# Seven weight blocks of a 1024x1024 layer pair at seven places modulo 512 bytes

## The chip, the core and the metric

The kernel runs on one core of a Trainium2 chip. The metric is device time in microseconds (us) of one execution; three runs of the kernel before gave 335.15, 336.11 and 336.05 us, so the median is 336.05. The profile is one further execution under the hardware profiler.

TensorE (PE in the profile) multiplies. Each of its matmuls has a stationary operand, which a separate LDWEIGHTS instruction reads from SBUF (engine PEld in the profile), and a moving operand, which streams out of SBUF while the matmul runs. VectorE is DVE, ScalarE is ACT, GpSimd is POOL; SP issues most of the small transfers and POOL those of the weights.

## What is computed

The input x is 8 batches of 256 rows of 256 values, with a context of 120 rows per batch.

```python
x = x + xattn(layernorm(x), ctx, ctx, ctx)      # gelu(x c^T) * (x c^T) @ c
n = layernorm(x)
h = silu(n @ w1.T * s1) * (n @ w2.T * s2)       # 256 -> 1024, twice
h = gelu(h @ h1.T * s_h1)                       # 1024 -> 1024
h = gelu(h @ h2.T * s_h2)                       # 1024 -> 1024
x = x + h @ w3.T * s3                           # 1024 -> 256
```

All five weight matrices are ternary (-1, 0, 1), with one scale for each output column. The 2048 rows are worked on as NT = 4 tiles of N = 512 rows, rows in the free dimension.

## The kernel before

**Stages.** Batch by batch, attention and the second layernorm give xT (lines 275 to 285 are its matmuls). `gated` (L438) multiplies xT by the stationary block `w12`. Then come four calls of `hidden` (L514), two for each 1024x1024 layer, each for two tiles of 512 rows; last `output` (L560) multiplies by `w3`, and finish_rows (L308, L309) scales and adds the residual.

**Exact activations.** An activation block is split in two fp32r parts, hi (rounded by ACT, L483) and lo = q - hi (DVE, L487), and each product is done twice, once with each part. In `operand` the two parts stand in a ring of RING = 3 slots: hi0, lo0, hi1, lo1 in the pool "middle", hi2, lo2 in the pool "later".

**Seven products instead of eight.** `hidden` is a 2x2 block scheme of the Strassen-Winograd kind. A layer's weight is four 512x512 blocks "11", "12", "21", "22" and three sums of them, s1, s2, s4, which DVE makes in place (`sum_weights`, L359). Each of these seven stationary blocks belongs to one of the seven products of ORDER, and lies in one of seven SBUF tiles `wt[0]` to `wt[6]`, named w0 to w6; HOME says which, for each layer. A tile is 128 partitions of 4x4x128 fp32 values, that is 8192 bytes on each partition. A product is 4 output groups `m` of 8 matmuls, 4 with hi and 4 with lo, each with a stationary slice of 128x128 and a moving slice of 128x512:

```python
def product(p, slot, m, bank):
    w = weight(layer, WEIGHT[p])
    for kind, part in enumerate(slot_views(slot)):
        for k in range(4):
            nc.tensor.matmul(
                mm[bank], lhsT=w[:, m, k, :], rhs=part[:, k, :],
                start=(p in OPENS and kind == 0 and k == 0),
                stop=(p in CLOSES and kind == 1 and k == 3), skip_group_check=True)
```

So a call has 7 x 4 x 8 = 224 matmuls, the four calls 896, and every weight tile is the stationary operand of 128 of them. In `output` the roles turn: slices of hi and lo are stationary, `w3` moves, 256 columns at a time.

**Order of the work.** Every operation goes into a `Plan` with an engine, a cost and its reads and writes; a list scheduler with fixed seeds (PICKS) sets the order on each engine before the program is built. It knows costs and dependences, not addresses. The loads of the second layer's blocks (L351, on POOL) wait until the products that read the tile before are done.

**Where the tiles lie.** The pool "keep" is filled in the order of its lines: q0 to q7 (8192 bytes each), w0 to w6, d0 to d3, w32; the pools of attention, and later "middle", begin behind it. "early" (w12, xT) and "later" (hi2, lo2, w3, o, x1) lie at the right end. Three constants pad: ALIGN = 16 fp32 values ahead of "keep", ALIGN_W3 = 8 ahead of w3, ALIGN_RIGHT = 112 at the end of "later". In the built program q0 starts at byte 8192 of a partition and w0 at 73728. Modulo 512 bytes, which this text calls the *place* of a tile (a stationary slice of 128 fp32 values is 512 bytes, a moving slice of 512 is 2048, so all slices of a tile share its place):

| tiles | place before |
|---|---|
| w0 to w6 | 0 for all seven |
| hi0, hi1, hi2, lo0, lo1, lo2 | 0 |
| w12 and xT | 480 |
| w3 | 32 |
| d0 to d3 | 0; `bad`, with which DVE combines them (L379), 384 |

Of the kernel before, what the change touches and what calls it, by code (L numbers as in the profile page):

```python
# [10 lines left out]
F32 = mybir.dt.float32  # L11
F32R = mybir.dt.float32r
# [8 lines left out]
P = 128  # L21
# [21 lines left out]
)  # L43
ALIGN, ALIGN_W3, ALIGN_RIGHT = 16, 8, 112
ATT, LOADS = 4, 6
FORCE_GENERAL = False

FIRST = (range(2), range(2, 4))
# [125 lines left out]
def xattn_ffn_kernel(ctx: ExitStack, tc: tile.TileContext, x, ctx_b, wall, scal, s3, out):  # L174
# [137 lines left out]
    with ExitStack() as es, ExitStack() as wide:  # L312
        open_pool = lambda stack, name, **kw: stack.enter_context(
            tc.tile_pool(name=name, bufs=1, **kw))
        keep = open_pool(es, "keep")
# [3 lines left out]

        mm = [psum.tile([P, N], F32, name=f"mm{i}") for i in range(8)]  # L320
        q = [keep.tile([P, 4, N], F32, name=f"q{i}") for i in range(8)]
        wt = [keep.tile([P, 4, 4, P], F32R, name=f"w{i}") for i in range(7)]
        d = [keep.tile([P, 1024], BF16, name=f"d{i}") for i in range(4)]
        w32 = keep.tile([P, 1024], F32, name="w32")
        x1s = dram.tile([NB * S, D], F32, name="x1s")
# [274 lines left out]
        for c in (0, 2):  # L600
            plan.dma("POOL", 0.8, lambda c=c: load_w12(c), 1.05, r=[("first", 0, 0)],
                     w=[("w12", c), ("w12", c + 1)], chain="weights")
# [80 lines left out]

    with tc.If(inexact == 0 if FORCE_GENERAL else inexact != 0):
        with ExitStack() as es:
# [8 lines left out]
            for c in range(NCH):  # L694
                w = wpool.tile([P, 1024], F32, tag=f"g{c}", name=f"g{c}")
# [90 lines left out]
```

## Time and profile before

| | before |
|---|---|
| median of 3 runs | 336.05 us |
| the profiled execution's own time | 334.57 us |
| its span, first to last instruction | 332.7 us |
| mean granted TensorE clock | 0.990 |
| PE busy | 318.5 us, 96% |
| PEld busy | 274.0 us, 82% |
| DVE busy | 257.5 us, 77% |
| ACT busy | 214.8 us, 65% |
| POOL busy | 52.8 us, 16% |

Busy time of PE is the union of pipelined matmuls: a matmul with 512 moving columns is shown as 389 ns long, though the next one starts well before its end. What a matmul costs in a dense stretch is the distance from start to start, and this text calls it the *pitch*. It is had by dividing a stretch's length by the number of matmuls in it. The chain of work that ended last gives such stretches with their counts.

### The profile page before, as it was taken

The page shows a single profiled execution, that of the slowest core. Times are in us where ns is not written, and L with a number is a line of the kernel's source. Part 1 is how long each engine was busy: PE and PEld are TensorE (multiplying, and loading weights), DVE is VectorE, ACT ScalarE, POOL GpSimd, SP SyncE. Part 2 cuts the span into 40 slices and gives each one's busy share as a digit, 9 for nine tenths or more (in the row PEclk, how much of TensorE's full clock was granted, in tenths as well). Part 3 has the DMA queues.
Part 4 walks back from the last instruction along what each step waited for, and adds up shares of the span by engine and source line. Part 5 has one row for each costly group of instructions (what it writes and reads, how often), then busy time and mean ns, then how long its engine had stood idle before and what let it go on. Part 6 is the DMA issues. An engine that isn't in the chain of part 4 may idle for free.

```text
span 332.7 us, 4563 instructions
## 1 busy us (share of the span) xinstructions
PE 318.5 (96%) x1670; PEld 274.0 (82%) x1670; DVE 257.5 (77%) x410; ACT 214.8 (65%) x316; POOL 52.8 (16%) x93
## 2 busy tenths in 40 slices
PE   3599999999999999999999999999999999999993
PEld 2399999988888888888888888888888888889993
DVE  5777778788998758997577998966997855747984
ACT  2457777558389777676777875688668656664510
POOL 4273141020015031111012210022003000000000
PEclk9989999999999999999999999999999999999997
DMA  7969700020059519509848860019006200002542
GB/s 220 384 204 340 254 33 33 32 95 3 0 176 115 58 10 149 97 14 223 204 97 221 122 155 9 0 12 109 8 0 69 27 0 2 0 0 66 146 126 87
DMA packets 22382, 32.44 MB, mean 97 GB/s; under 512 B 1744, under 2 KB 15184, under 8 KB 22352
## 3 DMA queue, kind: packets, MB, share of 16 engines
q0 software_dynamic: 10256, 17.30, 27.9%
q1 hardware_dynamic: 12096, 14.77, 14.3%
q8 instruction: 15, 0.25, 0.3%
q14 instruction: 15, 0.12, 0.1%
HBM read 33.64 MB, written 4.19 MB: 114 GB/s over the span
## 4 chain that ended last, share of the span: by engine, by line
PE 95%; DVE 1%; POOL 1%; DMA 1%; issue 0%; SPq 0%; ACT 0%; POOLq 0%
PE mm L514 61%; PE mm L438 18%; PE mm L560 9%; PE mm L275 2%; PE mm L285 2%; PE mm L280 2%; POOL ln_rs L252 1%; DMA xb<-x_d 1%; DVE ln_st L241 0%; DVE xn L263 0%; DVE o L308 0%; DVE xb L301 0%; DVE o L309 0%; DVE ge L298 0%; SPq L207 0%
## 5 line engine op out<-in xcount | busy, mean ns | idle before, releaser
L514 PE MATMUL mm<-hi,w 128*128 128x512 f32 x448 | 119.7, 389 | 0.0
L514 PE MATMUL mm<-lo,w 128*128 128x512 f32 x448 | 119.7, 389 | 0.0
L487 DVE TENSOR_TENSOR lo<-q,hi 128x1024 fp32r<-128x1024 f32 x72 | 86.3, 1220 | 17.1 <-ACT hi L483 17.0
L514 PEld LDWEIGHTS mm<-lo,w 128*128 128x128 f32 x448 | 84.1, 188 | 17.5
L514 PEld LDWEIGHTS mm<-hi,w 128*128 128x128 f32 x448 | 84.1, 188 | 17.4
L483 ACT CAST hi<-q 128x1024 fp32r<-128x1024 f32 x72 | 72.7, 1046 | 11.1 <-PE mm L560 8.2
L438 PE MATMUL mm<-xT,w 128*128 128x256 f32 (+1 forms) x384 | 65.8, 326 | 0.0
L438 PEld LDWEIGHTS mm<-xT,w 128*128 128x128 f32 x384 | 56.5, 191 | 5.4
L529 DVE TENSOR_TENSOR q<-q,mm 128x512 f32<-128x512 f32 x48 | 32.9, 687 | 28.7 <-PE mm L514 27.7
L533 ACT ACTIVATE q<-q,sc 128x512 f32<-128x512 f32 x48 | 34.2, 722 | 23.2 <-DVE q L529 22.8
L377 POOL DMA_DIRECT2D d<-wall_d x22 | 24.6, 1141 | 118.8 <-ACT d L375 118.8
L523 ACT COPY q<-mm 128x512 f32<-128x512 f32 x48 | 28.1, 587 | 22.8 <-PE mm L514 21.9
L459 ACT ACTIVATE q<-mm,sc 128x256 f32<-128x256 f32 (+1 forms) x48 | 25.9, 546 | 19.3 <-PE mm L438 19.0
L506 DVE TENSOR_TENSOR q<-q,q 128x1024 f32<-128x1024 f32 x32 | 38.2, 1218 | 0.0
L461 DVE SCALAR_TENSOR_TENSOR q<-q,sc,mm 128x256 f32<-128x256 f32 (+1 forms) x48 | 26.3, 560 | 3.6 <-ACT q L459 2.1
L375 ACT ACTIVATE d<-w 128x1024 bf16<-128x1024 f32 x22 | 23.0, 1057 | 0.0
L359 DVE TENSOR_TENSOR w<-w,w 128x512 fp32r<-128x512 f32 x32 | 20.8, 683 | 0.0
L560 PE MATMUL mm<-w,hi 128*128 128x256 f32 x128 | 20.2, 280 | 0.0
L560 PE MATMUL mm<-w,lo 128*128 128x256 f32 x128 | 20.1, 279 | 0.0
L275 PE MATMUL mm<-ident,xn 128*128 128x128 f32 x64 | 11.2, 298 | 7.7 <-DVE xn L263 7.7
L560 PEld LDWEIGHTS mm<-w,hi 128*128 128x128 f32 x128 | 17.2, 188 | 0.1
L560 PEld LDWEIGHTS mm<-w,lo 128*128 128x128 f32 x128 | 17.2, 188 | 0.0
(47 smaller groups left out, 181.0 us busy)
## 6 DMA issues: line engine op xcount, KB each, us to landing
w<-wall_d POOLq DMA_DIRECT2D x11, 1024.0 KB, 8.8
d<-wall_d POOLq DMA_DIRECT2D x22, 256.0 KB, 6.3
w<-wall_d SPq DMA_DIRECT2D x8, 512.0 KB, 4.0
x<-x1s SPq DMA_DIRECT2D x16, 128.0 KB, 2.8
out_d<-o SPq DMA_DIRECT2D x16, 128.0 KB, 1.9
cb<-ctx_d SPq DMA_DIRECT2D x8, 248.0 KB, 5.7
xb<-x_d SPq DMA_DIRECT2D x7, 256.0 KB, 7.2
x1s<-xb SPq DMA_DIRECT2D x7, 256.0 KB, 2.9
```

Of the source, the lines that this page charges most:

```text
L377: plan.dma("POOL", 0.8, lambda: nc.gpsimd.dma_start(d4, src, accum_op=ALU.add), 1.04, w=[("d", i)], lag=8.0)
L438: nc.tensor.matmul(sides[side], lhsT=w12[:, m // 2, (((m % 2) * 2 + side) * 2 + k) * P :][:, :P], rhs=xT[t % 2][i][:, k, cols], start=firs ...
L459: add("ACT", act(n, 1), lambda o=o, b0=b0, m=m: nc.scalar.activation(o, b0, AF.Silu, scale=sc[:, m : m + 1]), r=[("mm", banks[0]), "sc", " ...
L461: add("DVE", dve(n) + 0.05, lambda o=o, b1=b1, m=m: nc.vector.scalar_tensor_tensor(o, o, sc[:, 8 + m : 9 + m], b1, op0=ALU.mult, op1=ALU.m ...
L483: nc.scalar.copy(slot_views(i)[0][:, ms], q[src][:, ms])
L487: nc.vector.tensor_sub(l[:, ms], q[src][:, ms], h[:, ms].bitcast(F32))
L506: add("DVE", dve(1024), lambda ms=ms: nc.vector.tensor_tensor(q[into][:, ms], q[x][:, ms], q[y][:, ms], op=ALU.subtract), r=q_keys(x, ms) ...
L514: nc.tensor.matmul(mm[bank], lhsT=w[:, m, k, :], rhs=part[:, k, :], start=(p in OPENS and kind == 0 and k == 0), stop=(p in CLOSES and kin ...
L523: add("ACT", act(512), lambda: nc.scalar.copy(q[i][:, m], mm[bank]), r=[key], w=[("q", i, m)])
L529: add("DVE", dve(512), lambda: nc.vector.tensor_tensor(o(), o(), mm[bank], op=ALU.add), r=[key], w=[("q", i, m)])
L533: add("ACT", act(512, 1), lambda: nc.scalar.activation(o(), src(), AF.Gelu, scale=sc[:, col : col + 1]), r=["sc", "table"] + ([] if p in a ...
L560: nc.tensor.matmul(mm[banks[j]][:, :D], lhsT=part[:, k, j * P : (j + 1) * P], rhs=later["w3"][:, r, k * D : (k + 1) * D], start=(r == 0 an ...
```

## The change

The tiles w0 to w6 get small pads ahead of them, so that their places modulo 512 bytes become 0, 64, 128, 192, 256, 320 and 448. A last pad of 64 bytes fills up to 512, so that every tile behind them moves by exactly 512 bytes and keeps its place.

```diff
 ATT, LOADS = 4, 6
+OFF = (0, 64, 128, 192, 256, 320, 448)
 ...
         q = [keep.tile([P, 4, N], F32, name=f"q{i}") for i in range(8)]
-        wt = [keep.tile([P, 4, 4, P], F32R, name=f"w{i}") for i in range(7)]
+        wt = []
+        for i, off in enumerate(OFF):
+            if off:
+                keep.tile([P, (off - OFF[i - 1]) // 4], F32, name=f"off{i}")
+            wt.append(keep.tile([P, 4, 4, P], F32R, name=f"w{i}"))
+        keep.tile([P, (512 - OFF[-1]) // 4], F32, name="off7")
         d = [keep.tile([P, 1024], BF16, name=f"d{i}") for i in range(4)]
```

The order of the instructions on all five engines, and what they wait for, is the same in both programs; only addresses differ. The pads are never written or read.

## The prediction

> **What bounds the kernel now.** I read the chain of work that ended last first, since PE is busy 96% of the span and the question is what a matmul costs. From 63 us it reads:
>
> ```profile
> 63.15 3.64 PE mm L438 x16
> 66.79 0.86 PE mm L285 x4
> 67.66 5.47 PE mm L438 x24
> 73.13 0.44 PE mm L275 x4
> 73.57 1.86 PE mm L438 x8
> 75.43 0.44 PE mm L275 x4
> 75.86 18.18 PE mm L438 x80
> 94.04 203.12 PE mm L514 x896
> 297.16 22.40 PE mm L560 x192
> ```
>
> Columns: start, length in us, engine and line, number of instructions. The 896 matmuls that read the moved blocks are one unbroken piece of 203.12 us, 61% of the span: PE waits for nothing in it, and a matmul costs its pitch, 203.12 / 896 = 226.7 ns. The 80 matmuls of the same shape in L438 take 227.2 each, the eight ahead of them 1.86 / 8 = 232.5. L560, with half as many columns, takes 22.40 / 192 = 116.7 ns; L438 with 256 columns, from an earlier piece of the same chain, 4.79 / 40 = 119.8:
>
> ```profile
> 42.64 4.79 PE mm L438 x40
> ```
>
> The timeline of PE at the seam of L438 and L514 (start, length, then form and count):
>
> ```profile
> 93.64 0.40 PE L438 MATMUL mm<-xT,w 128*128 128x512 f32 x1
> 93.88 1.08 PE L514 MATMUL mm<-hi,w 128*128 128x512 f32 x4
> 94.80 1.08 PE L514 MATMUL mm<-lo,w 128*128 128x512 f32 x4
> 95.72 1.07 PE L514 MATMUL mm<-hi,w 128*128 128x512 f32 x4
> 96.62 1.07 PE L514 MATMUL mm<-lo,w 128*128 128x512 f32 x4
> ```
>
> Starts 0.92, 0.92, then 0.90 us apart for four: the first eight cost (95.72 - 93.88) / 8 = 230 ns, the later ones 226. Nothing is waited for here. What differs is one passage: while the last L438 matmul streams from place 480, the first slice of w0, at place 0, is being loaded. The next eight have hi0, lo0 and w0 all at 0 and still need a while to find the steady pitch. The last view is the group of that line:
>
> ```profile
> L514 PEld LDWEIGHTS mm<-hi,w x448: 187/188/188, 93.6 to 295.6; 128*128 128x128 f32 x150
> L514 PE MATMUL mm<-hi,w x448: 387/389/398, 93.9 to 295.9; 128*128 128x512 f32 x150
> ```
>
> Minimum, median, maximum in ns. A long one shows a long pitch: the 398 belongs to those first eight. So the trace holds unsettled matmuls from 2 ns under to 9 ns over the steady ones.
>
> **The change part by part.** No instruction, wait, queue entry or DMA is added, removed or reordered; only addresses change. So the sum has one main term: matmuls of L514 times the change of their pitch. w0 keeps place 0; six tiles move, each stationary in 4 calls x 4 groups x 8 = 128 matmuls, 768 in all. While such a matmul streams hi or lo from place 0, the next slice of the same tile is loaded from place 64 to 448 instead of 0. Every ns on each is 0.768 us on the path.
>
> Does the pitch depend on the place? A rule of the Trainium skill speaks against it. SBUF — State Buffer, section SBUF: two separate sides, says that among the engines only VectorE and GpSimd contend for a port, while PE has its own and never waits; TensorE: Matmul & The Clock Gate, section Back-to-back issue gap, gives the isolated gap as columns / 2.4 GHz plus 2.5 ns, 216 ns for 512 and 109 for 256. By these the sum is zero. The trace does not agree: 226.7 and 119.8 ns are 11 ns over either figure, and for one shape, 256 columns, there are two steady pitches, 119.8 with both operands at 480 and 116.7 with w3 at 32 moving against hi and lo at 0. Instruction type, columns, and clock are alike; the places differ. One row also speaks for the rule: L280, plain fp32, reads its stationary slice from six tiles with six different places, and its groups of four stay at 0.86 us. But each entry there takes 0.86 / 4 = 215 ns for 256 columns, so it streams at about half the rate, and a shared resource would have room. I take the fp32r rows, as they are the same kind as L514.
>
> How large, and which sign? From both sides:
> - Best row: the +32 byte lead of w3 saves 119.8 - 116.7 = 3.1 ns. On 768: -2.4 us. Should the pitch fall to L280's 215 ns, which are 2 x 256 steps at half rate (226.7 - 215 = 11.7), -9.0 us.
> - Unsettled rows: the first eight of L514 cost 230 - 226.7 = +3.3 ns, the eight of L438 232.5 - 226.7 = +5.8 (this piece includes a change of instruction kind at its end), the longest single one +9. On 768: +2.5, +4.5 and +6.9 us.
>
> I take the unsettled rows, midway between 3.3 and 5.8: 4.6 ns x 768 = +3.5 us. They have 512 columns, as L514 has, and one of them follows directly on a passage between unequal places; the w3 row has 256 columns, the other operand moving, and a distance (32) that the change does not use. In the changed kernel each of the 28 products also begins with a new place, so the steady state is left 28 times where it is now left once; that is inside the 4.6 ns.
>
> The other readers and writers of the tiles I cost at nothing:
> - L359, the 32 block sums on DVE, now has operands at three places. Nearest row: L379 combines `bad` at 384 with d at 0 over equally many 32-bit words in 686 ns, against 683 for L359 with all at 0. At 3 ns each that is 0.1 us, on an engine that is 77% busy. The lo parts that DVE owes to PE are ready 8.7 to 17 us ahead of the matmul (the trace's ends of L487 against the starts of L514), and that slack covers it.
> - L375 on ACT reads two slices each 1059 ns; the same slack covers it.
> - L351, the eight 1 MB loads, lands 8.0 us after issue (median; worst 15.4). The last is issued at 188.75 and feeds sums at 196.00 and a product at 202.7. A shifted destination might lengthen it; below 6 us nothing shows, and PE, if slower, gives it more time.
>
> Against the profiled execution: 334.57 us, 1.9 of it outside the span of 332.7. The change falls in the span: 334.6 + 3.5 = 338.1. The three runs have their median 1.5 us above the profiled one; I add the same +3.5 to that: 339.6 us.
>
> **The rivals.**
> - *A place that helps (faster).* The place of the stationary slice behind or ahead of the moving one decides how long the two streams hold each other up, and equal places are a bad case. For: L560, the only steady fp32r row with unequal places, is the quickest. Against: the passage from 480 to 0 (the moving one 32 bytes short of the stationary one) was followed by slower matmuls, not quicker. It decides for faster once the mean pitch over the six moved tiles is under 226.7. Price: 3.1 ns on all six, 336.05 - 2.4 = 333.6; with the whole excess gone, 327. The operands could follow in either case: they are ready 8.7 us early at the least, and DVE is busy 157.5 of the 203 us.
> - *No effect.* The skill's rule holds for L514, or tiles that gain and tiles that lose cancel: 336.05. For: L280. Against: the two pitches of 256 columns, and six tiles at six distances cancelling to under 1 us (1.3 ns on the mean) would be luck.
> - *A heavier conflict (slower by much).* Some distances lock into a state worse than any seen in passing, say 12 ns on all six: +9.2, 345 us. Nothing in the trace shows such a row; its longest is +9.
> - That the change does not do what it says is excluded: the built program has the tiles at these places and everything else where it was.
>
> **How the numbers follow.** Slower by the unsettled pitch, 339.6 (337.2 to 343, from +2 to +9 ns): 0.56. Heavier conflict, above 343: 0.10. Helping place: 0.26, most of it between 332.5 and 335, less below. No effect within 0.3% (1.0 us, about what a measurement of this kernel tells from no change): 0.08. So faster 0.26, same 0.08, slower 0.66. The range, 332.5 to 346.0, takes in the mild gain and most of the heavier conflict; outside stay a gain of over 3.5 us and a loss of over 10. As signs are mixed: the likeliest case alone has 337.2 to 343.
>
> **What would show it.** Right: the L514 piece of the chain grows from 203.12 to about 206.6 us with still 896 matmuls and no wait in it, all pieces before and after keep their lengths, and the timeline shows products of w0 (the first, and those of its three other calls) at 0.905 us for four and those of moved tiles at about 0.925, each tile with a pitch of its own. The helping place shows groups of four under 0.905 us for at least some tiles. Wrong altogether: all 28 products at 0.905 with the time unchanged; or new idle time of PE in L514, ended by DVE, ACT or a landing weight block, which would put the cost in L359 or L351 and not in the pitch.

## The result, and the profile after

The changed kernel is slower by about 1%: median 339.65 us of 8 runs (337.73 to 340.48) against 335.97 us (335.15 to 336.55). The ratio is 1.0106, with a 95% interval of 1.0084 to 1.0128. The profiled execution took 337.73 us, 3.16 more than that of before, and is the fastest of the eight. The granted clock was 1.00 from 105 to 290 us in this trace and in all the others of this text, so the pitches can be compared directly.

The chain of work that ended last, from the same point as before (start, length in us, engine and line, count; L444, L520 and L566 are L438, L514 and L560 of before):

```profile
73.57 1.86 PE mm L444 x8
75.42 0.44 PE mm L276 x4
75.86 18.18 PE mm L444 x80
94.04 206.35 PE mm L520 x896
300.39 22.40 PE mm L566 x192
322.79 0.12 PE mm L682 x2
322.90 7.68 PE mm L566 x64
```

From 40 to 94.04 us the pieces of the two chains agree to 10 ns, and the output stage is 22.40 and 7.68 us as before. All of the difference is in one piece: 896 matmuls take 206.35 instead of 203.12 us, +3.23. They are still one unbroken piece, so no wait has been added; the matmuls follow each other more slowly.

The timeline of PE in the changed kernel shows where. Each line below is the first group of a product, so the distance to the next line is a product of 32 matmuls. The tiles come in the order w0, w1, w4, w5, w6, w2, w3, and w0 again (w0's first product starts at 93.88):

```profile
93.88 1.08 PE L520 MATMUL mm<-hi,w 128*128 128x512 f32 x4
...
101.16 1.09 PE L520 MATMUL mm<-hi,w 128*128 128x512 f32 x4
...
108.62 1.09 PE L520 MATMUL mm<-hi,w 128*128 128x512 f32 x4
...
115.90 1.10 PE L520 MATMUL mm<-hi,w 128*128 128x512 f32 x4
...
123.37 1.09 PE L520 MATMUL mm<-hi,w 128*128 128x512 f32 x4
...
130.71 1.09 PE L520 MATMUL mm<-hi,w 128*128 128x512 f32 x4
...
138.13 1.08 PE L520 MATMUL mm<-hi,w 128*128 128x512 f32 x4
...
145.46 1.09 PE L520 MATMUL mm<-hi,w 128*128 128x512 f32 x4
...
152.73 1.09 PE L520 MATMUL mm<-hi,w 128*128 128x512 f32 x4
```

(108.62 - 101.16) / 32 = 233.1 ns for w1, and so on. Taken from the starts of all 128 matmuls of each tile (one product in each of the four calls):

| tile | w0 | w1 | w2 | w3 | w4 | w5 | w6 |
|---|---|---|---|---|---|---|---|
| place | 0 | 64 | 128 | 192 | 256 | 320 | 448 |
| pitch before, ns | 226.9 | 226.7 | 226.7 | 226.7 | 226.7 | 226.7 | 226.7 |
| pitch after, ns | 227.2 | 233.3 | 232.4 | 229.0 | 227.8 | 233.3 | 229.1 |

Each tile has a pace of its own, and it is the same within 0.9 ns in all four of its products. There is a pattern: 64 and 320 agree, 192 and 448 agree, 256 is close to 0. Places 256 bytes apart behave alike.

### The profile page after: what moved, and what is told of

Its sections match the earlier page's. It is cut to its first block, busy times and chain, and to the rows that moved or that the text cites. A ratio compares the mean times of both kernels' runs of the same rounds, so it can differ in the third digit from the quotient of the medians.

```text
span 335.9 us, 4563 instructions
## 1 busy us (share of the span) xinstructions
PE 321.7 (96%) x1670; PEld 274.1 (82%) x1670; DVE 257.8 (77%) x410; ACT 215.1 (64%) x316; POOL 52.9 (16%) x93
## 4 chain that ended last, share of the span: by engine, by line
PE 95%; DVE 2%; POOL 1%; DMA 1%; issue 0%; ACT 0%; POOLq 0%
PE mm L520 61%; PE mm L444 18%; PE mm L566 9%; PE mm L276 2%; PE mm L286 2%; PE mm L281 2%; POOL ln_rs L253 1%; DMA xb<-x_d 1%; DVE ln_st L242 1%; DVE xn L264 0%; DVE o L309 0%; DVE xb L302 0%; DVE o L310 0%; DVE ge L299 0%; DVE ln_ve L248 0%
## 5 line engine op out<-in xcount | busy, mean ns | idle before, releaser
L520 PE MATMUL mm<-hi,w 128*128 128x512 f32 x448 | 121.4, 393 | 0.0
L520 PE MATMUL mm<-lo,w 128*128 128x512 f32 x448 | 121.3, 392 | 0.0
L520 PEld LDWEIGHTS mm<-hi,w 128*128 128x128 f32 x448 | 84.2, 188 | 19.0
L520 PEld LDWEIGHTS mm<-lo,w 128*128 128x128 f32 x448 | 84.2, 188 | 19.0
L444 PE MATMUL mm<-xT,w 128*128 128x256 f32 (+1 forms) x384 | 65.9, 326 | 0.0
L444 PEld LDWEIGHTS mm<-xT,w 128*128 128x128 f32 x384 | 56.5, 191 | 5.4
L365 DVE TENSOR_TENSOR w<-w,w 128x512 fp32r<-128x512 f32 x32 | 20.8, 685 | 0.7 <-DMA w<-wall_d 0.7
L566 PE MATMUL mm<-w,hi 128*128 128x256 f32 x128 | 20.2, 280 | 0.0
L566 PE MATMUL mm<-w,lo 128*128 128x256 f32 x128 | 20.1, 279 | 0.0
L566 PEld LDWEIGHTS mm<-w,hi 128*128 128x128 f32 x128 | 17.3, 188 | 0.1
L566 PEld LDWEIGHTS mm<-w,lo 128*128 128x128 f32 x128 | 17.3, 188 | 0.0
```

The costliest lines, as they stand in the source:

```text
L444: nc.tensor.matmul(sides[side], lhsT=w12[:, m // 2, (((m % 2) * 2 + side) * 2 + k) * P :][:, :P], rhs=xT[t % 2][i][:, k, cols], start=firs ...
L520: nc.tensor.matmul(mm[bank], lhsT=w[:, m, k, :], rhs=part[:, k, :], start=(p in OPENS and kind == 0 and k == 0), stop=(p in CLOSES and kin ...
L566: nc.tensor.matmul(mm[banks[j]][:, :D], lhsT=part[:, k, j * P : (j + 1) * P], rhs=later["w3"][:, r, k * D : (k + 1) * D], start=(r == 0 an ...
```

## The experiments

In what follows the *distance* is the place of the stationary slice minus that of the moving one. The theory to be tested is that the pitch follows from the distance alone, repeating every 256 bytes. Code cuts leave out lines where "..." stands. The rivals were that the weight's own place counts, and that the cost comes from changing place at the seams between products.

**Move the other operand.** The weight tiles stay as in the changed kernel; hi0 to lo2 go from place 0 to 448. The diff is against the changed kernel.

```diff
-ALIGN, ALIGN_W3, ALIGN_RIGHT = 16, 8, 112
+ALIGN, ALIGN_W3, ALIGN_RIGHT = 16, 24, 112
 ...
+            pool1.tile([P, 112], F32, name="off_hi")
             later["hi"] = [pool1.tile([P, 4, N], F32R, name=f"hi{i}") for i in range(2)]
```

> The weight tiles stay at 0, 64, 128, 192, 256, 320, 448; hi0 to lo2 move from place 0 to 448. Theory 1 (the pitch follows the distance, weight place minus hi/lo place): the distances become 64, 128, 192, 256, 320, 384, 0 for w0 to w6, so the pitches of the changed kernel move along: w0 233.3 ns, w1 232.4, w2 229.0, w3 about 227.5, w4 233.3, w6 226.7; w5, at 384, a distance not yet seen, 232.4 if the pattern repeats every 256 bytes. L520 then takes about 206.6 us and the time is about 339.5 to 340 us, unless the output stage, whose distance changes from 32 to 96, changes too (up to 5 ns x 256 = 1.3 us). Rival (the weight's own place counts, 0 and 256 being good): the pitches by tile stay as they were, w0 226.7, w1 233.3, w6 229.1.

Measured, w0 to w6: 233.2, 232.5, 229.1, 227.0, 233.3, 232.6, 227.6 ns. The pitches have moved along by one tile, as the distances have; w0, which nobody touched, went from 227.2 to 233.2 because its partner moved. And w6, now at the same place as its partner, comes back to the good pace after some matmuls. The timeline has the starts of w0 and of the product after it, and then those of w6 and some groups on:

```profile
95.00 1.09 PE L520 MATMUL mm<-hi,w 128*128 128x512 f32 x4
...
102.46 1.09 PE L520 MATMUL mm<-hi,w 128*128 128x512 f32 x4
...
124.80 1.09 PE L520 MATMUL mm<-hi,w 128*128 128x512 f32 x4
...
130.28 1.07 PE L520 MATMUL mm<-hi,w 128*128 128x512 f32 x4
131.19 1.07 PE L520 MATMUL mm<-lo,w 128*128 128x512 f32 x4
132.10 1.08 PE L520 MATMUL mm<-hi,w 128*128 128x512 f32 x4
```

(102.46 - 95.00) / 32 = 233.1 ns for w0, where the changed kernel has (101.16 - 93.88) / 32 = 227.5; the last groups of w6 are 0.91 us apart, 227 for each matmul. The rival with the weight's own place is out. The piece of 896 takes 206.76 us, and the output stage, now at another distance, 23.04 + 7.88 us, 0.84 more than before:

```profile
95.16 206.76 PE mm L520 x896
301.93 23.04 PE mm L566 x192
324.96 0.12 PE mm L683 x2
325.08 7.88 PE mm L566 x64
```

The ratio to before is 1.0163 (1.0123 to 1.0202), some 5.3 us at the medians. The two stages account for 3.64 + 0.84 = 4.5; in this profile the stage ahead of them also ended 1.1 us later (95.16 against 94.04), which other executions show without any change there, as the runs below do.

**No seams.** All seven weight tiles at 64. The diff is against the kernel before.

```diff
+        keep.tile([P, 16], F32, name="off")
         wt = [keep.tile([P, 4, 4, P], F32R, name=f"w{i}") for i in range(7)]
+        keep.tile([P, 112], F32, name="off7")
```

> All seven weight tiles at place 64, hi and lo at 0. Theory 1 (distance): every tile has the 233.3 ns that w1 has at 64, the L514 piece takes 896 x 233.3 = 209.0 us instead of 203.1, and the time is 336.0 + 5.9 = about 341.9 us. Rival (seams: matmuls are unsettled because the place changes with each product): all products alike, so one settling and then 226.7 ns, 336 us.

```profile
95.47 209.07 PE mm L516 x896
```

209.07 / 896 = 233.3 ns, the same for all seven tiles, and 341.81 us, ratio 1.0188 (1.0143 to 1.0232). Nothing changes place here between products, and the cost is there in full. So it is a steady state of that distance, not a failure to settle. The starts of single matmuls show what this state looks like: here they are by turns 231 and 236 ns apart, at 192 in the changed kernel they repeat 226, 229, 232, and at distance 0 they repeat 227, 227, 226. So the mean pitches of this text are means of such cycles, not the pitch of each matmul.

**Only seams.** The tiles alternately at 0 and 256, against the kernel before:

```diff
+        wt = []
+        for i in range(7):
+            if i:
+                keep.tile([P, 64], F32, name=f"off{i}")
+            wt.append(keep.tile([P, 4, 4, P], F32R, name=f"w{i}"))
-        wt = [keep.tile([P, 4, 4, P], F32R, name=f"w{i}") for i in range(7)]
```

> Weight tiles alternately at 0 and 256 (w0 0, w1 256, w2 0, ...), hi and lo at 0. Theory 1 with a period of 256 bytes: all products settle at 226.7 ns; only some ns are lost at the seams between products, at most what w4 lost in the changed kernel (1.1 ns x 896 = 1.0 us), so 336.0 to 337.0 us. Rival with a period of 512 bytes: the tiles at 256 keep a worse pitch all through, and w4's 227.8 was not settling but its own pace.

```profile
76.84 18.18 PE mm L442 x80
95.02 203.12 PE mm L518 x896
298.14 19.61 PE mm L564 x168
```

203.12 us as before to the hundredth, w0 at 226.9 and the others at 226.7 ns, ratio 1.0006 (0.9988 to 1.0024). Jumps of 256 bytes at the seams cost nothing. The 1.1 ns that w4 lost at place 256 in the changed kernel were its predecessor's doing (w1 at 64 in the first layer, w2 at 128 in the second): it took six to nine matmuls to find back to the good pace.

**The distances between.** Seven other places, in the changed kernel:

```diff
-OFF = (0, 64, 128, 192, 256, 320, 448)
+OFF = (0, 32, 96, 160, 224, 288, 384)
```

> Weight tiles at 0, 32, 96, 160, 224, 288, 384, to fill in the distances between the seven that are known. Theory 1 with period 256: 288 like 32, 384 like 128 (232.4 ns), 0 at 226.7; the new ones 32, 96, 160, 224 are not foretold, but if the output stage's 32-byte lead of the moving operand (3.1 ns less) holds for 512 columns, 224, which is 32 short of 256, is under 226.7: about 223 to 224 ns. Rival (equal places are the best there is): no tile under 226.7.

Measured: 227.9, 233.1, 234.0, 233.4, 233.4, 233.3 and 232.2 ns. 288 is like 32 and 384 like 128, as the period says. No tile is under 226.7; the distance 224, from which the output stage has its 116.7 ns, is among the worst for 512 columns. The lines have the starts of the first products of w1 at 32, w4 at 224 and w5 at 288:

```profile
102.62 1.09 PE L520 MATMUL mm<-hi,w 128*128 128x512 f32 x4
...
110.08 1.10 PE L520 MATMUL mm<-hi,w 128*128 128x512 f32 x4
...
117.55 1.09 PE L520 MATMUL mm<-hi,w 128*128 128x512 f32 x4
```

That is 233.1 ns at 32 and 233.4 at 224. This kernel, the two of the next experiment and the one after them ran once each; what is read from them are pitches, not their times.

**Finer steps.** In two kernels the weight tiles are cut from slightly larger ones, so that single fp32 values can be stepped; w12's chunks and w3's halves get gaps, for other distances with 256 columns. The diff is against the kernel before; the values of the second kernel stand in the comments.

```diff
-ALIGN, ALIGN_W3, ALIGN_RIGHT = 16, 8, 112
+ALIGN, ALIGN_W3, ALIGN_RIGHT = 16, 16, 72      # second: 16, 40, 48
+OFF = (0, 4, 8, 16, 240, 248, 252)      # second kernel: (0, 12, 20, 24, 232, 244, 236)
 ...
-        wt = [keep.tile([P, 4, 4, P], F32R, name=f"w{i}") for i in range(7)]
+        wt = [keep.tile([P, 2048 + 64], F32R, name=f"w{i}")[:, o // 4 :][:, :2048].rearrange(
+            "p (m k c) -> p m k c", m=4, k=4) for i, o in enumerate(OFF)]
+        keep.tile([P, 64], F32, name="off7")
 ...
-        w12 = early_pool.tile([P, 4, 1024], F32R, name="w12")
+        w12 = early_pool.tile([P, 4, 1024 + 56], F32R, name="w12")[:, :, :1024]      # second: 8
 ...
-            later["w3"] = pool2.tile([P, 2, 1024], F32R, name="w3")
+            later["w3"] = pool2.tile([P, 2, 1024 + 16], F32R, name="w3")[:, :, :1024]
```

> A finer look around the good distances, to see whether any beats distance 0. Distance is the stationary slice's place minus the moving one's, modulo 256. w0 to w6 at 0, 4, 8, 16, 240, 248, 252 (hi and lo at 0). In the output stage w3's halves at 64 and 128 (distances 192 and 128); in the gated stage w12's four chunks at distances 128, 96, 64, 32 from xT. Theory 1 (a narrow good spot at 0): small distances already cost part of the 6.4 ns that 32 costs, all w1 to w6 between 227 and 233 ns, and no tile under 226.7. Rival (distance 0 is only near the best): one of 4 to 16 or 240 to 252 is below 226.5 ns. For 256 columns: the output stage was 116.7 ns at 224 and 120.0 at 160 (run with hi and lo at 448); at 192 and 128 I expect between these, 117 to 120 ns, and in the gated stage 120 ns or slightly less at its four new distances.

> The same with w0 to w6 at 0, 12, 20, 24, 232, 244, 236; w3's halves at distances 96 and 32, w12's chunks at 128, 160, 192, 224. Theory 1: w1 to w6 between 228 and 234 ns, the further from 0 the nearer to 233. Rival: one is below 226.5 ns. For 256 columns: w12's chunk at 224 repeats the output stage's 116.7 ns if the distance alone decides, and stays near 120 if the roles of the tiles do; 512 columns at 224 in the gated stage repeat 233.4.

The mean pitch with 512 columns from these two kernels and those above, distance modulo 256 (the distance 0 is that of the kernel before):

| distance | 0 | 4 | 8 | 12 | 16 | 20 | 24 | 32 | 64 | 96 |
|---|---|---|---|---|---|---|---|---|---|---|
| ns | 226.7 | 232.5 | 230.7 | 226.8 | 233.2 or 226.7 | 233.2 | 230.5 | 233.1 | 233.3 | 234.0 |

| distance | 128 | 160 | 192 | 224 | 232 | 236 | 240 | 244 | 248 | 252 |
|---|---|---|---|---|---|---|---|---|---|---|
| ns | 232.4 | 233.4 | 229.0 | 233.4 | 231.1 | 231.6 | 227.2 | 233.3 or 226.7 | 233.2 | 226.8 |

Two things had not been expected: the pitch doesn't rise evenly with the distance (12, 240 and 252 are good, 4 and 248 are not), and two distances have two values. At 16 the tile w3 of the first of these kernels runs at 233.2 ns in its products of the first layer, where w2 at 8 comes ahead of it, and at 226.7 in the second layer, where w6 at 252 does. From the timeline of PE, the first three groups of four of each:

```profile
139.24 1.10 PE L517 MATMUL mm<-hi,w 128*128 128x512 f32 x4
140.18 1.09 PE L517 MATMUL mm<-lo,w 128*128 128x512 f32 x4
141.11 1.10 PE L517 MATMUL mm<-hi,w 128*128 128x512 f32 x4
...
227.64 1.07 PE L517 MATMUL mm<-hi,w 128*128 128x512 f32 x4
228.55 1.07 PE L517 MATMUL mm<-lo,w 128*128 128x512 f32 x4
229.46 1.07 PE L517 MATMUL mm<-hi,w 128*128 128x512 f32 x4
```

Starts 0.935 us apart in the one, 0.91 in the other: same line, same tile, same instruction. At 244 (w5 of the second kernel) it is the same: 233.3 ns in three products, 226.7 in the one that follows a tile at 226.8. So there is a good pace of 226.7 ns; distances 0, 240 and 252 came to it also after a slower product, 16 and 244 keep it if they are given it, and others, such as 4, 32 and 64, leave it even after a good product. None goes below it. The 80 matmuls of 512 columns in the gated stage, with other tiles on both sides, slow down as well when w12's chunks leave distance 0:

```profile
76.63 18.66 PE mm L441 x80
...
75.82 18.61 PE mm L441 x80
```

The first line is from the first kernel (chunks at 128, 96, 64, 32), the second from the second (128, 160, 192, 224); before it was 18.18 us.

With 256 columns the order is another one. The output stage had 118.6 ns at 192 and 118.5 at 128, 119.2 at 96, 118.3 at 32 and 120.0 at 160 (the kernel with hi and lo at 448), against 116.7 at 224 and 119.8 at 0 (gated stage). w12's chunk at 224 in the gated stage had a median of 117 ns, so the quicker row of the profile before did not depend on the tile.

**Whose partner is it?** A slice is loaded while the matmul ahead of it streams: in the trace of before each load in L514 starts 2 to 4 ns after the start of the matmul ahead. It could be that the loaded slice has to fit the one streaming at that time, or that it has to fit its own moving slice. One tile, w0, got slices that keep one of these distances while the other takes four values; hi and lo got k slices at 0, 64, 128, 192. The loads of w0 are split in four for this, which the cut below leaves out. The diff is against the kernel before.

```diff
-        wt = [keep.tile([P, 4, 4, P], F32R, name=f"w{i}") for i in range(7)]
+        w0 = keep.tile([P, 4, 592], F32R, name="w0")[:, :, :576].rearrange(
+            "p m (k c) -> p m k c", k=4)[:, :, :, :P]
+        wt = [w0] + [keep.tile([P, 4, 4, P], F32R, name=f"w{i}") for i in range(1, 7)]
 ...
-            later["hi"] = [pool1.tile([P, 4, N], F32R, name=f"hi{i}") for i in range(2)]
+            later["hi"] = [pool1.tile([P, 4, N + 16], F32R, name=f"hi{i}")[:, :, :N] for i in range(2)]
 ...
```

> Which two slices have to fit: a matmul's own stationary and moving slice, or the moving slice that streams and the stationary slice that is loaded meanwhile for the next matmul. The four k slices of hi and lo lie at 0, 64, 128, 192 modulo 256. In w0 the k slices advance by 64 too, and its four groups m begin at 0, 64, 128, 192; so in group m every matmul's own distance is 64 m, and the distance to the next slice 64 m + 64 (the last matmul of each group of eight apart, which meets the next group's first slice). The other tiles keep all slices at one place. Theory A (next): the four groups of w0 have 233.3, 232.3, 229.0 and 226.7 ns. Theory B (own): 226.7, 233.3, 232.3 and 229.0 ns. w1 to w6 meet four distances in turn under both and should be near 231 ns. The loads of w0 are split in four and the output stage's distances change too, so the total time decides nothing here.

Measured for the four groups of w0: 229.1, 230.4, 232.1, 231.3 ns, and 231.7 for the other tiles. That is neither list. The slice streaming alone can't decide, as the first group would then be the slowest and it is the fastest; the own distance has the fastest group right, but not the slowest (it foretold the second, and it is the third), nor the sizes. The 231.7 ns of the other tiles, which meet four distances in turn, is also more than the 230.3 that the four have on the mean by the table. With groups of only eight matmuls at one distance the state left by the group before may cover both. This stays open.

**The version that the map points to.** No distance tried is better than 0 for 512 columns, so the map has no better places for the weight tiles than those of before. The gated stage of tiles t = 0 and 1 has 256 columns and stood at 0; here it gets 224, and the rest stays. The diff is against the kernel before.

```diff
-        xT = [[early_pool.tile([P, 2, N], F32R, name=f"xT{i}{j}") for i in range(2)] for j in range(2)]
+        xT_raw = [[early_pool.tile([P, 2 * N + 64], F32R, name=f"xT{i}{j}") for i in range(2)] for j in range(2)]
+        xT = [[v[:, 8 * (t < HALVED) :][:, : 2 * N].rearrange("p (k c) -> p k c", k=2)
+               for v in xT_raw[t % 2]] for t in range(NT)]
 ...
```

> The kernel before, with xT of the halved tiles t = 0 and 1 (256 moving columns) 32 bytes further on, so that its distance to w12 becomes 224, which gave 117 ns in the middle for 256 columns instead of 120; tiles t = 2 and 3 (512 columns) and the weight tiles keep distance 0. Theory (distance, best place depends on the number of columns): 256 matmuls x 3 ns = 0.8 us less at most, perhaps half of it as attention's matmuls break the stretches up: 335.2 to 335.7 us against 336.0. Rival (256 columns gain only in an unbroken stretch): no change.

The unbroken stretch of 40 matmuls that took 4.79 us before, in the chain of this kernel:

```profile
42.87 4.67 PE mm L440 x40
```

116.8 ns each instead of 119.8. From the first matmul of the gated stage to the first of the hidden products it is 75.13 us in this trace and 75.72 in that of before, 0.59 less. The median is 334.90 us (22 runs) against 335.71 (27), the ratio 0.9984 (0.9968 to 0.9999): half a microsecond by the ratio, just clear of zero.

## Why the prediction was right, and where it was right for another reason

- *The bound.* That L514 is one unbroken piece in which every ns per matmul counts in full held: +3.23 us there, and the pieces from 40 us on and after it unchanged.
- *The main term.* The six moved tiles cost 230.8 ns on the mean, +4.15 against the +4.6 taken; 768 x 4.15 = 3.19 us. With 0.04 for w0 that is the piece's 3.23. The medians differ by 3.7, about half a microsecond more; the profiled execution is the fastest of its kernel, and what the others add was not traced.
- *Where the 4.6 ns came from.* The prediction took it from matmuls that had not settled. This was the wrong picture with the right size. With all tiles at 64 there is nothing to settle, and the pace is 233.3 ns steadily. The eight unsettled matmuls of before happened to be of the size at which other distances stay. Nor do the moved tiles share one pitch: they run from 1.2 ns over the good pace (w4 at 256, which goes back to it) to 6.6 (w1 and w5), and 4.15 is the mean over the six places that happened to be chosen. That it lies near 4.6, and the median within 0.1 us of the 339.6 foretold, is luck.
- *The seams.* "The steady state is left 28 times" was not a cost of its own: jumps of 256 bytes cost nothing. What is lost at a seam depends on the distance left: w0 had 227.2 ns instead of 226.9 and w4 227.8 instead of 226.7, after products at worse distances.
- *The rule of no contention.* The two pitches of 256 columns were the right row to hold against it. The distance decides, together with the pace before at a few distances, and moving the other operand alone shows it.
- *The helping place.* It fell at the step from the output stage to L514: the 32-byte lead saves 3 ns with 256 columns and costs 6.8 with 512 (233.4 ns). The prediction had set it aside for having 256 columns and the other operand moving. The columns were the reason; the roles were not, as 224 is just as quick with w12 stationary and xT moving (116.8 ns).
- *No effect.* No tile gained, so there was nothing to cancel with.
- *The heavier conflict.* No distance tried cost over 7.3 ns.
- *A slip in the sum.* +2 ns on 768 matmuls are 1.5 us, so the likeliest case began at 337.6 us and not at 337.2. Nothing hangs on it.
- *The terms set to nothing.* L359 (L365 after) is at 685 ns against 683, and no wait of PE appears. One block sum of DVE waits 0.7 us for a weight load, far ahead of its product.

## What to carry to other kernels

When matmuls run without a gap, compare their pitch between lines of the same shape before anything else; two steady values for one shape at the same granted clock mean that something else sets it, and addresses are a candidate that no order of instructions and no wait will show. In this kernel, the start of the stationary and of the moving slice should differ by a multiple of 256 bytes for fp32r matmuls of 512 columns, and by 32 short of one (the moving slice 32 bytes further on) for 256 columns; pads of a few hundred bytes in the pools decide 1 to 2% of the time. A pad or a new small tile ahead of the operands can undo it by accident, so the places are worth a look after each change of layout.

## What the runs showed of the hardware

- The pitch of 512-column fp32r matmuls depends on the distance of the two slices' starts modulo 256 bytes: 226.7 ns on the mean at 0, 229.0 at 192, 232.4 at 128, 233 to 234 at 32, 64, 96, 160 and 224.
- At two of the distances next to 0 two paces exist for one and the same code, and the product ahead decides between them: 226.7 or 233.2 ns at 16 bytes, 226.7 or 233.3 at 244.
- The best distance depends on the number of columns: with 256, 224 gives 116.7 ns and 0 gives 119.8.
- A product that is slow on the mean is a repeating pattern of single pitches: 231 and 236 ns by turns at 64, 226, 229 and 232 at 192.
- What in the chip makes the pitch depend on the distance, and whether the pair that counts is that of one matmul or of two in succession, the runs do not tell.
